# Issuing the attention work beside the FFN by a clock kept while tracing, in an adaLN block on one Trainium2 core

## The chip, the core and the metric

The kernel runs on one core of one Trainium2 chip. The metric is the device time of one execution in microseconds (us). The profile is one execution taken by the hardware profiler. Engines in it: PE (TensorE, matrix products; PEld are its weight loads), DVE (VectorE), ACT (ScalarE), POOL (GpSimd) and SP (SyncE, which here only issues DMAs). Each engine runs its own queue in order; semaphores order engines among each other. In the code they are `pe`, `dve`, `act`, `pool` and `sp`.

## What is computed

The reference, cut to what matters. `x` is 4 x 2048 x 256 (four batches, 2048 positions, 256 features), float32:

```python
mod = silu(c) @ wmod                      # sa, ca, ga, sb, cb, gb per batch
ga, gb = sign(.) * max(abs(.), 0.25)
h = layernorm(x) * (1 + ca) + sa
x = x + ga * attn(h)
h = layernorm(x) * (1 + cb) + sb
x = x + gb * ffn(h)

def ffn(x):                               # weights hold -1, 0, 1
    h = silu(x @ w1.T * w1_s) * (x @ w2.T * w2_s)     # 256 -> 1024
    h = gelu(h @ h1.T * h1_s)                         # 1024 -> 1024
    h = gelu(h @ h2.T * h2_s)
    return h @ w3.T * w3_s                            # 1024 -> 256

# attn: 4 heads of 64, chunks of 64 positions; per chunk and head
A = inv(I + strict(wk @ wk.T * decay))    # wk: unit keys, moved by one position
v_new = A @ v - (A @ wk) @ S
o = (rk * g**p) @ S + intra @ v_new
S = g**64 * S + (wk * g**(63-p)).T @ v_new
return h + (alpha * o) @ Wr.T
```

The state S makes the 32 chunks a chain: a chunk's output, and so its FFN input, needs all chunks before it.

## The kernel before, in words

**Steps and pairs.** A step `s` is one chunk of 64 positions of all four batches and all heads (32 steps); a pair `g` is two steps (16 pairs). The FFN runs over a pair at once (512 columns); in pair 0 it runs over each step by itself (256 columns).

**FFN** (`class Ffn`, L456). `gated` (L511), 8 rounds: four products of PE with `fw1`, four with `fw2` (resident weights) into two PSUM tiles `ps`, Silu on ACT (`sg`), a product on DVE (`raw`). `hidden` (L527), 2 layers of 8 units: 16 products with a weight `w` (512 KB, fetched from DRAM into a ring of three tiles), then Gelu on ACT (`raw`). `last` (L540): 64 products with the resident `fw3`, giving `ps3`; DVE multiplies by gb (`gb`), `store` (L563) adds to `y` and writes out. All activations are split into a rounded part and the rest (`split`, L428: a cast on ACT, a subtraction on DVE or POOL, both written to `act`), so every product is made twice, once with each part: 64 wide products in the gated part of a pair, 256 in the hidden units, 64 half as wide with w3. PSUM tiles of the FFN come from the pool `pf`, three tiles. `Ffn.run` is a generator that yields 88 times: 16 in the gated part, four for each of the 16 hidden units, 8 in the last part. A unit of the plan is the work between two yields.

**Attention, local part** of a step, which needs only x: `load` (DMA of `y`), `local_hidden` (layer norm into `hid`, a square `sq`), `local_sizes` and `local_units` (norms `rn`, unit keys `rk`), `local_residual`, `local_keys` (transposes `tp` on PE, copies `hT` and `keys` on ACT), `local_values` (PE `vp`), `local_reads` (`rkg`), `local_shift` and `local_writes` (`wkg`, by DMA). For a pair: `local_grams` (PE `G`; DVE makes `E` and `IT`; DMAs lay E out anew as `U`), 31 rows `local_inverse` on DVE (two instructions each, `zt` and `Z`), `local_blocks` (DMAs back to `E`), `local_diagonal` (DVE `Dm`), `local_merge1` (PE `yp`, ACT `Y`) and `local_merge2` (PE `ep`, ACT copies to `E`).

**Attention, recurrence** of a step: `rec_state` (PE `R` and `O`, DVE subtracts from `v`, ACT copies `oT`), `rec_values` (PE `V`, ACT `vn`), `rec_update` (PE `new`, DVE `S` and `oT`), `rec_out` (PE `ap`, DVE `ga`, POOL adds to `y`), `ffn_norm` (DVE `bs`, `mv`, `rs`, `xn`; POOL takes the root `rs`) and `ffn_turn` (PE transposes `tpf`, ACT `hm` in 8 instructions, split into `hs`, the input of the FFN). PSUM tiles of these come from two pools, `a2` (two tiles) and `a1` (one tile).

**What sets the order.** The program is traced once; a compile-time scheduler then places the instructions. `stage()` (L105) puts all that is traced inside it behind the last instruction recorded so far on each engine. A class `Engine` (L72) records each instruction in its one `call`, so every line of the profile except that of the set-up's weight check reads L82, and one goes by tile names. In `planned` (L770) each event of the attention is given a number of a unit by hand (`recur`, `local`, `later`); `steps` (L847) walks through the FFN's units and traces the events of a unit, each in a `stage()`, behind it. The FFN's own instructions are in no stage, so the scheduler may move them. The recurrence of pair g + 1 lies beside the FFN of pair g, the local part of later steps beside it too. All DMAs of this part, `w` included, are issued by SP, in one order.

**Set-up** (L572 to L765): loads, the weights' check and rearrangement (`inspect`, `layer`), the tables, and the local part and recurrence of the first steps; then a flag is read and a branch taken (`tc.If`, L871). The path run here is `exact`.

Of the kernel before, what the change touches and what calls it, by code (L numbers as in the profile page):

```python
# [41 lines left out]
C = 64  # L42
# [47 lines left out]
def adaln_block_kernel(ctx: ExitStack, tc: tile.TileContext, x_in, ww, wr, decay, log_alpha, w1, w2, h1, h2, w3, scol,  # L90
# [365 lines left out]
    class Ffn:  # L456
# [6 lines left out]
        def __init__(self, g, i, hs, fp, exact):  # L463
            self.steps, self.fp, self.exact = range(2 * g, 2 * g + 2) if i is None else (2 * g + i,), fp, exact
            self.n = len(self.steps) * B * C
            self.a = hs if i is None else hs[:, :, :, i * B * C:(i + 1) * B * C]
            self.parts = 2 if exact else 1
            self.next, self.new = None, []

        def run(self):  # L470
            for o in range(NH):
                yield from self.gated(o)
            for layer in range(2):
                for o in range(NH):
                    yield from self.hidden(layer, o)
            for i in range(len(self.steps)):
                for n in range(2):
                    yield from self.last(i, n)
# [4 lines left out]
        def fetch(self, src, o):  # L483
            t = self.ring(src.shape[0] // P)
            move(out=t, in_=src[:, o:o + P].rearrange("(k p) o -> p k o", p=P))
            return t
# [24 lines left out]
        def gated(self, o):  # L511
# [12 lines left out]
            self.done(o, to, pool if o < NH - 2 else dve)  # L524
            yield

        def hidden(self, layer, o):  # L527
            ps = pf.tile([P, self.n], F32, tag="f", name="ps2")
            if self.exact:
                w = self.ring(NH)  # L530
                move(out=w.bitcast(F32), in_=fhs[layer][o])
            else:
                w = self.fetch((h1, h2)[layer], o * P)
            yield from self.product(ps, w, 4)
            to = self.acts(o)
            act.activation(to, ps, AF.Gelu, scale=sc[:, 2 + layer, o:o + 1])
            self.done(o, to)
            yield

        def last(self, i, n):  # L540
            if n == 0:
                self.ps = pf.tile([P, 2, D], F32, tag="f", name="ps3")
            at_ = slice((2 * i + n) * P, (2 * i + n + 1) * P)
            for d in (0,) if self.exact else range(0, D, P):
                w = fw3 if self.exact else self.fetch(w3, d)
                count = NH * self.parts
                for m in range(count):
                    k, j = divmod(m, self.parts)
                    pe.matmul(self.ps[:, n, d:d + w.shape[2]], lhsT=self.a[:, k, j, at_], rhs=w[:, k, :],
                              start=m == 0, stop=m == count - 1)  # L550
                    if d == 0 and m == count // 2 - 1:
                        yield
            end = self.steps[i] == NS - 1
            if n == 1 or end:
                m = slice(n, n + 1) if end else slice(0, 2)
                t = ap.tile([P, 2, D], F32, tag="gb", name="gb")
                dve.tensor_tensor(t[:, m], self.ps[:, m], mod[:, GB, m], ALU.mult)
                self.new.append((self.steps[i], t, m))
                if end or self.steps[i] == NS - 2:
                    self.store(dve)  # L560
            yield

        def store(self, eng):  # L563
            s, t, m = self.new.pop(0)
            y = ys[s % 6]
            eng.tensor_tensor(y[:, m], y[:, m], t[:, m], ALU.add)
            for b in range(2):
                rows = out[b::2, s * C:(s + 1) * C, :].rearrange("q t d -> t q d")
                move(out=rows[:, m], in_=y[C * b:C * b + C, m])


    with tc.tile_pool(name="setup", bufs=1) as su:  # L572
# [62 lines left out]
        for h in range(2):  # L635
            move(out=wrT[C * (1 - h):C * (1 - h) + C, 1], in_=wr.rearrange("(k h p) o -> h p k o", h=2, p=C)[h])
        s3b = su.tile([P, D], F32, name="s3b")
# [34 lines left out]
        h0, h1_ = hid, su.tile([P, 2, D], F32, name="hid1")  # L672
# [16 lines left out]
        with stage():  # L689
# [5 lines left out]
            load(2)  # L695
            load(3)
# [11 lines left out]
        with stage():  # L708
# [5 lines left out]
            for j, to in ((2, GA), (5, GB)):  # L714
                for n in range(2):
# [4 lines left out]
                    raw = su.tile([P, D], F32, tag="raw", name="raw", bufs=4)  # L720
# [12 lines left out]
        with stage():  # L733
            for j in range(K - 1):
                local_inverse(j)
            local_residual(0, h0)
            local_residual(1, h1_)
        with stage():
            local_blocks()
        with stage():  # L740
            rn = local_sizes(local_hidden(2, hid))
            local_units(2, hid, rn)
# [6 lines left out]
            local_residual(2, hid)  # L749
# [7 lines left out]
        with stage():  # L757
            oT = rec_update(0, vn, None)
        with stage():
            rec_out(0, oT)  # L760
            ffn_norm(0, xn0)
        some = su.tile([1, 1], F32, name="some")
# [4 lines left out]
    NU = Ffn.UNITS  # L767
    FIRST = 2 * NU - Ffn.LAST

    def planned(exact, hs, fp):  # L770

        plan, had = {}, {"hs": hs}

        def add(u, what, *args, to=None):
            def do():
                got = what(*(had[a[1:]] if isinstance(a, str) else a for a in args))
                if to:
                    had[to] = got

            plan.setdefault(u, []).append(do)  # L780

        def turned(s):
            if s % 2 == 0:
                had["hs"] = new_hs(fp, exact)
            ffn_turn(s, had["xn"], had["hs"], exact)

        def later(u, n):

            for _ in range(n):
                u += 2 if u < FIRST else 1  # L790
            return u

        def recur(s, u):
            add(u, rec_values, s, to="vn")
            add(later(u, 3), rec_update, s, "=vn", "=oT", to="oT")
            add(later(u, 6), rec_out, s, "=oT")
            add(later(u, 10), ffn_norm, s, to="xn")
            add(later(u, 13), turned, s)

        def local(s, u, new=True):  # L800
            if new:
                add(u, local_hidden, s, hid, to="sq")
                add(later(u, 3), local_sizes, "=sq", to="rn")
                add(later(u, 4), local_units, s, hid, "=rn")
                add(later(u, 9), local_residual, s, hid)
            add(later(u, 7), local_shift, s)
            add(later(u, 8), local_keys, s, hid, to="hT")
            add(later(u, 11), local_values, s, "=hT")
            add(later(u, 11), local_reads, s)
            add(later(u, 12), local_writes, s)  # L810

        add(0, rec_state, 1, to="oT")
        recur(1, 8)
        local(2, -12, False)
        u = 4
        for g in range(1, NP):
            a, b = 2 * g, 2 * g + 1

            if g > 1:
                u = later(merge, 6)  # L820
                add(max(u - 18, 0), load, a)
                add(max(u + 2, 0), load, b)
                local(a, u)
                u = later(u, 11)
            local(b, u)
            add(later(u, 12), local_grams)
            u = later(u, 21)
            for j in range(K - 1):
                add(later(u, j // 2 if g == 1 else j * 2 // 3), local_inverse, j)
            u = later(u, K // 2 if g == 1 else (K - 2) * 2 // 3 + 1)  # L830
            add(u, local_blocks)
            merge = max(later(u, 11), FIRST + NU * (g - 2) + 10)

            m = merge
            add(m - 4, rec_state, a, to="oT")
            add(m - 1, local_diagonal)
            add(m, local_merge1, to="Y")
            add(later(m, 3), local_merge2, "=Y")
            recur(a, later(m, 6))
            add(later(m, 12), rec_state, b, to="oT")  # L840
            recur(b, later(m, 16))
        return plan, had

    def new_hs(fp, exact):
        return fp.tile([P, NK, 2 if exact else 1, N], FR if exact else F32, tag="hs", name="hs", bufs=1)

    def steps(exact):  # L847
        for e in engines:
            e.last = None
        with tc.tile_pool(name="ffn", bufs=2) as fp:  # L850
            hs = new_hs(fp, exact)
            with stage():
                ffn_turn(0, xn0, hs, exact)
            plan, had = planned(exact, hs, fp)
            u, f = 0, None
            for g, i in [(0, 0), (0, 1)] + [(g, None) for g in range(1, NP)]:
                before, f = f, Ffn(g, i, had["hs"], fp, exact)
                for n, _ in enumerate(f.run()):
                    if before and n == 17:
                        with stage():  # L860
                            before.store(pool)
                    if i is None and g < NP - 1 and n == NU - 2:
                        with stage():
                            f.store(pool)
                    for what in plan.pop(u, ()):
                        with stage():
                            what()
                    u += 1
            assert not plan, plan
# [33 lines left out]
```

## Time and profile before

| | us |
|---|---|
| median of 3 runs (lowest, highest) | 1963.68 (1962.59, 1964.57) |
| profiled execution, whole | 1957.66 |
| profiled execution, span from first to last instruction | 1955.8 |
| set-up, up to the first product `ps<-hs,fw` | 123.06 |
| pair 0 (two halves) | 123.06 to 263.39 |
| pairs 1 and 2 | 263.39 to 483.24 |
| pairs 3 to 13 | 483.24 to 1755.71 |
| pair 14 | 1755.71 to 1863.55 |
| pair 15, with the last stores | 1863.55 to 1955.8 |

A pair is counted from its first gated product (`ps<-hs,fw`) to that of the next. In the profile's groups a line reads: line, engine, operation, output tile <- input tiles, shapes, count, and in square brackets the idle time of the engine before it with the tile of the instruction that ended it. In the list of waits the numbers are us in total, times, longest. In tables by stretch of time come for PE, PEld, DVE, ACT and POOL the busy us (and instructions), then the granted clock of PE (1.00 is full), the share of the DMA engines' time, and GB/s.

### The profile page before, as it was taken

How to read it: one execution, taken by the hardware profiler on the slowest of the kernel's cores; microseconds unless marked ns; L12 is line 12 of the kernel's file. 1: busy time of each engine (PE TensorE's matmuls, PEld its weight loads, DVE VectorE, ACT ScalarE, POOL GpSimd, SP SyncE). 2: the span in 40 equal slices, each digit the busy share in tenths (PEclk: the TensorE clock that was granted, in tenths of full speed). 3: DMA queues.
4: the chain of work that ended last, by engine and by line, in shares of the span. 5: the costliest groups of instructions: out<-in, count | busy, mean ns of one | idle time of the engine just before them, and what ended most of it. 6: DMA issues, size and time to landing. Idle time of an engine off the chain costs nothing.

```text
span 1955.8 us, 37975 instructions
## 1 busy us (share of the span) xinstructions
PE 1731.8 (89%) x15572; PEld 1405.4 (72%) x15572; DVE 1023.3 (52%) x2426; ACT 813.8 (42%) x1467; POOL 509.2 (26%) x474
## 2 busy tenths in 40 slices
PE   5278889998998989899898998989889898989998
PEld 3068877787776867778676776867778686777876
DVE  3536574555647365564635547363564736456322
ACT  4234444444444344444434334444444444444342
POOL 2222331504124140422404132240412314041020
PEclk7679899999999999999899999999999898999999
DMA  8815535242332425243252423415243252523322
GB/s 281 239 48 188 152 98 151 66 141 71 101 121 76 136 55 139 70 109 116 52 147 67 114 92 87 130 44 151 77 113 94 74 139 52 140 70 101 107 76 88
DMA packets 192216, 213.92 MB, mean 109 GB/s; under 512 B 112864, under 2 KB 147808, under 8 KB 192032
## 3 DMA queue, kind: packets, MB, share of 16 engines
q1 hardware_dynamic: 188096, 199.86, 36.4%
q10 hardware_dynamic: 3936, 11.54, 1.6%
q8 instruction: 125, 2.05, 0.4%
q14 instruction: 59, 0.48, 0.1%
HBM read 177.79 MB, written 25.17 MB: 104 GB/s over the span
## 4 chain that ended last, share of the span: by engine, by line
PE 56%; DVE 14%; DMA 9%; ACT 6%; POOL 4%; SPq 3%; issue 2%; DVEq 0%; POOLq 0%; ACTq 0%
PE ps L82 47%; ACT hm L82 4%; DMA w<-fh 3%; SPq L82 3%; DMA U<-d 3%; DVE Z L82 2%; DVE zt L82 2%; DVE raw L82 2%; DVE xn L82 2%; DMA wkg<-rk 1%; PE vp L82 1%; POOL rn L82 1%; PE new L82 1%; DVE E L82 1%; PE V L82 1%
## 5 line engine op out<-in xcount | busy, mean ns | idle before, releaser
L82 PE MATMUL ps<-act,w 128*128 128x512 f32 (+1 forms) x4352 | 992.2, 384 | 39.3 <-DMA w<-fh 25.9
L82 PEld LDWEIGHTS ps<-act,w 128*128 128x128 f32 x4352 | 780.6, 190 | 202.2 <-ACT act L82 16.7
L82 DVE TENSOR_TENSOR act<-raw,act 128x512 fp32r<-128x512 f32 (+1 forms) x306 | 204.4, 670 | 454.8 <-ACT act L82 436.0
L82 ACT ACTIVATE raw<-ps,sc 128x512 f32<-128x512 f32 (+1 forms) x272 | 178.8, 664 | 448.8 <-PE ps L82 424.3
L82 PE MATMUL ps<-hs,fw 128*128 128x512 f32 (+1 forms) x1088 | 299.0, 432 | 67.7 <-ACT hs L82 33.3
L82 PEld LDWEIGHTS ps<-hs,fw 128*128 128x128 f32 x1088 | 217.6, 214 | 138.9 <-DVE raw L82 44.3
L82 ACT CAST act<-raw 128x512 fp32r<-128x512 f32 (+1 forms) x408 | 240.6, 595 | 129.7 <-DVE raw L82 122.3
L82 POOL TENSOR_TENSOR rn<-rn,half 128x8 f32<-128x8 f32 x32 | 52.6, 1644 | 718.6 <-DVE rn L82 718.6
L82 POOL TENSOR_TENSOR act<-raw,act 128x512 fp32r<-128x512 f32 (+1 forms) x102 | 125.3, 1235 | 249.9 <-ACT act L82 249.9
L82 DVE TENSOR_TENSOR zt<-Z,U 128x126 f32<-128x126 f32 (+22 forms) x496 | 147.8, 298 | 44.7 <-DMA U<-d 32.1
L82 DVE TENSOR_TENSOR Z<-Z,zt 128x126 f32<-128x126 f32 (+22 forms) x496 | 156.2, 315 | 13.5
L82 PE MATMUL ps<-fw,act 128*128 128x256 f32 x1024 | 133.2, 285 | 2.1 <-DVE gb L82 2.0
L82 PEld LDWEIGHTS ps<-fw,act 128*128 128x128 f32 x1024 | 126.5, 189 | 4.6 <-DVE gb L82 2.2
L82 DVE SCALAR_TENSOR_TENSOR raw<-ps,sc,sg 128x512 f32<-128x512 f32 (+1 forms) x136 | 97.1, 715 | 55.2 <-PE ps L82 30.2
L82 ACT ACTIVATE sg<-ps,sc 128x512 f32<-128x512 f32 (+1 forms) x136 | 90.1, 662 | 82.8 <-PE ps L82 82.0
L82 POOL TENSOR_TENSOR rs<-rs,half 128x2 f32<-128x2 f32 x64 | 53.7, 839 | 208.4 <-DVE rs L82 194.1
L82 ACT ACTIVATE hm<-tpf,modT 128x64 f32<-128x64 f32 x256 | 79.4, 417 | 62.6 <-PE tpf L82 62.6
L82 ACT ACT_TABLE_LOAD x38 | 48.8, 1283 | 99.2 <-PE ps L82 90.0
L82 POOL TENSOR_TENSOR y<-y,ga 128x512 f32<-128x512 f32 x32 | 41.2, 1287 | 149.7 <-DVE ga L82 142.5
L82 DVE TENSOR_TENSOR hs<-hm,hs 128x512 fp32r<-128x512 f32 x32 | 26.0, 814 | 101.1 <-ACT hs L82 101.0
L82 PE MATMUL vp<-wwT,hT 128*128 128x256 f32 x256 | 65.1, 390 | 6.6 <-ACT hT L82 5.5
L82 DVE BATCH_NORM_STATS2 bs<-y 128x6 f32<-128x256 f32 x128 | 48.8, 417 | 37.9 <-POOL y L82 31.1
(198 smaller groups left out, 1465.7 us busy)
## 6 DMA issues: line engine op xcount, KB each, us to landing
w<-fh SPq DMA_DIRECT2D x272, 512.0 KB, 3.7
y<-in_x_dram SPq DMA_DIRECT2D x64, 128.0 KB, 4.2
st<-in_h_dram ACTq DMA_DIRECT2D x16, 512.0 KB, 7.2
U<-d SPq DMA_DIRECT2D x32, 256.0 KB, 4.4
fh<-st SPq DMA_DIRECT2D x16, 512.0 KB, 6.8
wkg<-rk SPq DMA_DIRECT2D x64, 126.0 KB
out_dram<-y SPq DMA_DIRECT2D x62, 128.0 KB, 2.4
d<-E SPq DMA_DIRECT2D x64, 64.0 KB, 1.9
```

What stands on the lines that cost most here:

```text
L82: made = make(*args, **kwargs)
```

## The change

The plan by hand goes. In its place, a class `Beside` keeps two clocks while the program is traced, `t` for PE and `dve` for VectorE. Each event has a list of what must be done before it, with a time that must have gone by since (`after`), and a cost on PE, a cost on DVE and the time for which it holds PSUM tiles (`COSTS`). After each unit of the FFN, whose cost is added to the clocks, every event that is ready by the clocks is traced, in the order of a list. The FFN's units are now in stages too, so their instructions stay where they are traced. `w` is issued by ACT, three units ahead (`stream`). `last` makes 14 of 16 products of both steps' first halves before those that need the last activations, and holds both `ps3` tiles at once; the last step is stored whole. In the set-up `load(2)` and `load(3)` come earlier, keys, values and shift of step 2 and hidden and units of step 3 are added, the ring `raw` has 2 tiles for 4, and the flag is read twice.

The diff, cut to its core:

```diff
+            if o > NH - 4:
+                self.stream(o - NH + 3)
             yield
+        def stream(self, m):
+            if self.exact and m < 2 * NH:
+                w = self.ring(NH)
+                self.coming.append(w)
+                act.dma_start(out=w.bitcast(F32), in_=fhs[m // NH][m % NH])
 
         def hidden(self, layer, o):
             ps = pf.tile([P, self.n], F32, tag="f", name="ps2")
-            if self.exact:
-                w = self.ring(NH)
-                move(out=w.bitcast(F32), in_=fhs[layer][o])
-            else:
-                w = self.fetch((h1, h2)[layer], o * P)
+            w = self.coming.pop(0) if self.exact else self.fetch((h1, h2)[layer], o * P)
             yield from self.product(ps, w, 4)
             to = self.acts(o)
             act.activation(to, ps, AF.Gelu, scale=sc[:, 2 + layer, o:o + 1])
             self.done(o, to)
+            self.stream(layer * NH + o + 3)
             yield
...
+        def last(self):
+            steps = range(len(self.steps))
+            ps = [pf.tile([P, 2, D], F32, tag="f", name="ps3") for i in steps]
+            most, count = (NH - 1) * self.parts, NH * self.parts
...
+            for i in steps:
+                if self.exact:
+                    some(i, 0, range(most))
+                yield
+                yield
+            for i in steps:
+                some(i, 0, range(most, count))
+                some(i, 1, range(count))
+                t = ap.tile([P, 2, D], F32, tag="gb", name="gb")
+                dve.tensor_tensor(t, ps[i], mod[:, GB], ALU.mult)
...
+    COSTS = {"state": (1.05, 0.7, (("a2", 2.4), ("a2", 2.4))), "merge1": (0.4, 0, (("a2", 2.2),)),
+             "merge2": (0.55, 0, (("a1", 2.4),)), "V": (0.5, 0, (("a2", 2.0),)), "update": (1.05, 1.7, (("a2", 3.2),)),
+             "out": (1.55, 0.7, (("a1", 2.9),)), "norm": (0, 2.0, ()), "turn": (0.45, 0.75, (("a1", 4.6),)),
+             "hidden": (0, 3.0, ()), "sizes": (0, 0.9, ()), "keys": (0.85, 0.2, (("a2", 3.0),)),
+             "values": (1.55, 0, (("a1", 3.0),)), "grams": (1.15, 2.8, (("a2", 4.2), ("a2", 4.2))),
+             "row": (0, 0.55, ()), "diag": (0, 1.3, ())}
+    class Beside:
...
+        def step(self, s):
+            self.add("state", s, rec_state, (s,), [("update", s - 1, 2.8), ("out", s - 1, 0), ("reads", s, 2.0)], "oT")
+            self.add("V", s, rec_values, (s,), [("merge2", s // 2, 2.8), ("state", s, 2.8), ("values", s, 3.0)], "vn")
+            self.add("update", s, rec_update, (s, "vn", "oT"), [("V", s, 2.5), ("writes", s, 1.5)], "oT")
+            self.add("out", s, rec_out, (s, "oT"), [("update", s, 3.2), ("residual", s, 3.5)])
+            self.add("norm", s, ffn_norm, (s,), [("out", s, 3.6), ("turn", s - 1, 0)], "xn")
+            self.add("turn", s, self.turn, (s, "xn"), [("norm", s, 4.5)] + ([("gated", s // 2 - 1, 0)] if s > 1 else []))
...
+        def ready(self, key, after):
+            if any((k, s) not in self.done for k, s, _ in after):
+                return None
+            t = max([self.done[k, s] + late for k, s, late in after], default=0.0)
+            if key[0] in ("row", "hidden"):
+                t = max(t, self.dve - 0.3)
+            tiles = [k for k, _ in COSTS.get(key[0], (0, 0, ()))[2]]
+            for k in set(tiles):
+                t = max(t, sorted(self.free[k])[tiles.count(k) - 1])
+            return t
...
+        def run(self, until=None):
+            while True:
+                soon = [(r, n) for n, e in enumerate(self.todo[:200]) if (r := self.ready(e[0], e[3])) is not None]
+                now = [n for r, n in soon if r <= self.t]
+                if now:
+                    self.issue(self.todo[now[0]])
+                elif until and until not in self.done:
+                    self.t = min(soon)[0]
+                else:
+                    return
...
+            for g, i in [(0, 0), (0, 1)] + [(g, None) for g in range(1, NP)]:
+                s = 2 * g + (i == 1)
+                beside.run(("turn", 2 * g + (i != 0)))
+                before, f = f, Ffn(g, i, beside.hs, fp, exact)
+                run, n = f.run(), 0
+                while True:
+                    with stage():
+                        if next(run, run) is run:
+                            break
+                    beside.passed(*f.cost(n))
...
+                    beside.run()
+                    n += 1
```

`issue` traces an event in a `stage()` and adds its costs to the clocks; `Ffn.cost` gives a unit 0.92 us on PE (half of it in pair 0) and 0.75 or 1.5 on DVE where it ends a product's chain.

## The prediction

> **What bounds the kernel now.** I read the busy table first, then who PE waits for, then PE in order of time over one pair, then the granted clock.
>
> ```profile
> PE 1731.8 (89%) x15572; PEld 1405.4 (72%) x15572; DVE 1023.3 (52%) x2426; ACT 813.8 (42%) x1467; POOL 509.2 (26%) x474
> ```
>
> PE is the bound, but 89% is an average: 11% of the span is PE idle. The waits of PE say behind what:
>
> ```profile
> PE ps L82 <- DVE raw L82: 42.8, 35, 2.8
> PE yp L82 <- DVE Dm L82: 36.0, 2, 35.1
> PE ps L82 <- ACT hs L82: 33.3, 15, 3.3
> PE tpf L82 <- DVE xn L82: 28.5, 25, 1.6
> PE ps L82 <- DMA w<-fh: 25.9, 16, 3.3
> ```
>
> The second is one wait in the set-up. The other four (130.5 us) return in every pair of steps, about 8.7 us each time. In time order, around the change from one FFN to the next:
>
> ```profile
> 1000.27 0.83 PE L82 MATMUL yp<-Dm,E 32*32 32x32 f32 x64
> 1001.03 5.30 PE L82 MATMUL ps<-act,w 128*128 128x512 f32 x22
> 1006.27 1.20 PE L82 MATMUL ep<-E,Y 32*32 32x32 f32 x64
> ...
> 1055.98 0.55 PE L82 MATMUL tpf<-kept,xn 128*128 128x128 f32 x3 [0.95 <-DVE xn L82]
> 1056.46 1.16 PE L82 MATMUL G<-keys 64*64 64x65 f32 x64
> 1059.75 0.73 PE L82 MATMUL ps<-hs,fw 128*128 128x512 f32 x2 [2.13 <-ACT hs L82]
> ...
> 1074.73 7.50 PE L82 MATMUL ps<-hs,fw 128*128 128x512 f32 x24 [2.04 <-DVE raw L82]
> 1082.89 11.18 PE L82 MATMUL ps<-act,w 128*128 128x512 f32 x48 [0.65 <-DVE raw L82]
> 1097.12 3.23 PE L82 MATMUL ps<-act,w 128*128 128x512 f32 x13 [3.05 <-DMA w<-fh]
> ```
>
> The recurrence (yp to tpf) begins in the FFN's ninth of 16 hidden units (3 + 87/16 after its first), takes 56 us, and its last transpose comes after the FFN's last product. So PE stands until xn, then hs, are there. Then the gated products wait for DVE, which runs rows of the inverse between them, and then a weight is late. The clock falls in such holes:
>
> ```profile
> 1016.00:1024.00 8.00, 8.00 (x96) 6.46 (x95) 3.62 (x7) 2.62 (x4) 1.45 (x1) 1.00 0.36 93
> 1056.00:1064.00 8.00, 5.63 (x79) 4.04 (x80) 4.27 (x7) 5.07 (x11) 3.94 (x6) 0.86 0.13 22
> 1072.00:1080.00 8.00, 5.96 (x19) 3.92 (x19) 7.62 (x19) 3.54 (x6) 2.79 (x3) 0.79 0.00 0
> 483.24:1755.71 1272.47, 1163.86 (x10472) 940.87 (x10473) 692.32 (x1618) 532.09 (x947) 350.46 (x320) 0.97 0.36 99
> ```
>
> (Third from last is the granted clock.) The last line is pairs 3 to 13, from first gated product to first gated product: 1272.47/11 = 115.7 us a pair.
>
> **The price of a dense pair.** Pair 15 has nothing beside it and gives the FFN alone:
>
> ```profile
> 1880.14 40.41 PE L82 MATMUL ps<-act,w 128*128 128x512 f32 x176
> 1939.00 5.86 PE L82 MATMUL ps<-fw,act 128*128 128x256 f32 x48
> ```
>
> 0.2296 us a wide product, 0.122 a w3 product. A pair has 64 + 256 wide and 64 of w3: 73.5 + 7.8 = 81.3 us. The events beside it: from 1000.27 to 1038.68 stand 121 wide products (27.8) and yp, ep, V, new, ap, R/O, tp, V, vp, so these nine cost 10.6 with their switches. From 1038.68 to 1050.09 stand 64 w3 products (7.8) and tpf, new, half a tp, ap: 3.6. Left are half a tp (0.4), vp (1.7), tpf (0.6), G (1.2), R/O (1.1): 5.0. Together 19.2, so 100.5 us a pair if PE never waits. Today's 115.7 has 15.2 on top: some 10 idle, the rest products stretched by waits and low clock.
>
> **Part by part.** *The order.* The changed kernel's issue order is visible. From pair 3 on PE has tp at unit 10, yp inside 10, ep at its end, V in 11, new, ap, R/O in 12, V and tp in 13, G and the first tpf behind 13, ap in 15, the second tpf after 28 of the 64 w3 products. After it come 36 x 0.122 = 4.4 us of work. The turn (hm 2.48, hs cast 0.62, handovers about 0.1 each) gives the first half of hs 3.3 us after tpf and the second (DVE 0.69) about 4.2. So both hs waits, the xn wait and the cold start go. What is late next, taken through the queues at those durations:
> - V waits for E, whose copy (1.16 in two, about 10 us into the unit 10 stretch) stands on ACT behind sq and Gelu: 0.5.
> - ap waits for oT; S and oT (0.87, 0.68) stand on DVE behind the unit's act: 0.5.
> - G needs both PSUM tiles of its pool. One is freed by S and oT of step b, behind xn of step a, which took 2.69 where POOL ran beside it (0.73 otherwise): 0 to 1.4, taken 1.4.
> - The first rows of the inverse stand on DVE ahead of hs. They need U, 8.8 us after E in the trace; some 10.8 after G, with 17 available: nothing, with 6 us of slack.
>
> *Rows in the gated part* are now one per pair of products: stt 0.75 + row about 0.5 in 1.84 us of PE, done before the POOL split starts, where zt and Z took 1.1 to 1.4 against 0.28. I cost them at 0; with that cover gone it is today's 2 to 4 us.
>
> *w on ACT, three ahead.* w leaves the SP queue, where a late y or wkg held it. Its issue stands on ACT between Gelu and cast: 13 in the hidden units. ACT's issues of the same 512 KB in the set-up took 0.34 and 0.45 alone, 0.66 each in four (2.63), 1.38 each in six (8.29). I take 0.5. At a layer's end the chain Gelu, issue, cast, DVE act is 0.25 + 0.69 + 0.5 + 0.62 + 0.69 + 0.1 = 2.9 against 14 products x 0.23 = 3.2 that don't need it: covered; at 1.38 it costs 0.6 twice. The first w of a pair is issued behind the sixth Silu, at about 11.4, lands at 3.7 (median) to 4.9, and is wanted at 14.7: 0.4 to 1.6, taken 0.6, at most today's 3.05. Boundaries and gb before its PSUM tile returns: 0.5.
>
> Waits: 0.5 + 0.5 + 1.4 + 0.6 + 0.5 = 3.5 (bounds 0.5 and 9). **A steady pair: 104.0.**
>
> *last()* computes 28 products before it needs the last act (3.4 us against 2.9): the wait goes.
>
> A rule beside the clock rows: the Trainium skill ("TensorE: Matmul & The Clock Gate", Part 1) has the array drop to half rate after about 3.4 us of idle and return after about as long of work. The trace agrees in kind: pair 15, started out of a 3.2 us wait, took 16.6 us for its 64 gated products instead of 14.7. By the rule, waits of half a microsecond keep the clock up; the sum above has that already.
>
> **The other stages.** Set-up: 123.06 us to the first FFN product. Work of steps 2 and 3 moves in. Hidden 2 lies partly in DVE's idle time before 63.5, where the rows still wait for the check of the weights; 1.7 us of it fall between rows, hidden 3 takes its old place, values 2 lie in PE's idle 4.7 before tpf. The second flag load is over long before. 123.5 (121 to 127).
> Pair 0 (140.3, in halves of 256 columns) is paced by w: a slot comes back with the last product, then Silu/Gelu 0.47, issue 0.5, landing 3.7 to 4.5, and 16 x 0.127 = 2.0: three units in 6.7 to 7.5, so 2.4 each. First half: gated 8 and its events 10, 16 x 2.4 = 38, rest 6: 62. Second: gated 10, nine units 21.6, seven at 2.0 with 15 of events, and its end 13 with the turn open: 74. Together **136** (129 to 142).
> Here the Trainium skill ("DMA: Bandwidth & Descriptors", "Issuing engines are not separate DMA queues") speaks against the move: an issue from another engine saves only issue time. If so and pair 0 kept its 140.3, the total would be 4 higher. The trace leaves it open, with w on one queue only.
> Pairs 1 and 2 still have a late second tpf: 100.5 + 3.5 + cold start 1.9 + open turn 4.3 = 110.2, and 2.1 open: 108.0. Pair 14 has no tp, vp, G: 100.5 - 6.1 + 3.5 + 4.3 = 102.2. Pair 15: 16.6 + 58.8 + 0.5 + 7.8, then gb, y and the store as today (7.3): 91.0.
> Sum: 123.5 + 136 + 110.2 + 108 + 11 x 104 + 102.2 + 91 = 1814.9 us of span. The profiled execution had 1.86 around its span (1957.66), and the median stands at 1963.68/1957.66 = 1.0031 of it: (1814.9 + 1.9) x 1.0031 = **1822 us**.
>
> **Rivals.**
> - *Nearly dense*: waits of 0.5 a pair, pair 0 at 131, set-up 121.5: 1773. For it: slack at U, hs, tp. Against: ACT and DVE are in order and the four waits above are each real queue positions.
> - *The clock kept in tracing runs ahead of the chip.* It counts 16.1 us of PE for events that cost 19.2 here, and no queues of ACT or POOL. PE then waits at more of the 17 events: 9 a pair instead of 3.5, pair 0 as today: 1904. Against: a clock that runs short on PE gives inputs more time, not less.
> - *Slower*: ACT becomes the bound. If an issue on ACT holds the engine until the transfer before it has drained, it costs about a landing, 3.7, and a unit takes 0.69 + 0.62 + 3.7 = 5.0 instead of 3.68: 13 x 1.33 = 17.3 a pair, 57 in pair 0, 2139 in all. It outweighs the gain of 11.7 from 3.3 us an issue. For it: 1.38 at six in a row; against: 0.34 to 0.66 otherwise, and w is issued one per 3.7 us.
> - *It moves nothing*: the holes close and open elsewhere for the same 115.7. Against: order and durations above leave no place for 15 us.
>
> **Chances.** Forecast (waits 2 to 5; 1800 to 1845) 0.55; nearly dense 0.15; clock ahead 0.20; moves nothing 0.04; ACT bound 0.06. A difference under 0.2% can't be told from no change here. Faster 0.90, same 0.02, slower 0.08. The range for 8 in 10 takes in most of the second and third case: 1778 to 1890.
>
> **What would show it.** hs and xn gone from PE's waits; gated products at 0.23; clock 1.00 through a pair; pairs at 102 to 106; w waits under 1 us; ACT issues near 0.5. Wrong if PE waits for E, oT or G's tiles by more than 2 us each, if DVE rows still hold raw, or if ACT queue time grows past 1 us an issue.

## The result, and the profile after

The kernel after takes 1868.41 us (median of 4 runs, 1866.87 to 1870.42); the kernel before, run beside it, 1963.13 (1961.39 to 1964.57). The ratio is 0.9518, with a 95% interval of 0.9502 to 0.9535: 4.8% faster. The forecast was 1822, the range 1778 to 1890. So the direction held and the size fell short by 46 us. The profiled execution took 1866.87, its span is 1865.1.

The busy table of the kernel after (busy us and share of the span for each engine):

```profile
PE 1704.2 (91%) x15572; PEld 1375.3 (74%) x15572; DVE 1002.9 (54%) x2424; ACT 816.8 (44%) x1467; POOL 528.5 (28%) x474
```

PE does the same 15572 instructions in 27.6 us less busy time, and its idle time falls from 224 to 161 us. The waits of PE over the whole span:

```profile
PE V L82 <- DVE v L82: 18.1, 13, 2.4
...
PE ps L82 <- ACT hs L82: 12.9, 5, 3.2
...
PE tpf L82 <- DVE xn L82: 7.8, 2, 6.4
```

The counts matter here: `hs` fell from 15 waits to 5 and `xn` from 25 to 2, all outside the ten steady pairs looked at below. In their place `V` waits, once a pair for `E` and once for `v`. By stages (pair 0, then pairs 3 to 13; third from last the granted clock):

```profile
124.58:280.69 156.11, 129.92 (x1524) 118.31 (x1524) 76.48 (x204) 67.30 (x154) 43.31 (x47) 0.91 0.44 131
...
501.82:1675.75 1173.93, 1134.71 (x10472) 912.29 (x10473) 678.97 (x1616) 533.86 (x947) 367.14 (x318) 1.00 0.39 107
```

Pairs 3 to 13, the steady pairs, take 1173.93/11 = 106.7 us each in place of 115.7, and the clock stays at 1.00. The gain is there: 11 x 9.0 = 99. Pair 14 (1675.75 to 1773.82) gives 9.8 more. Pair 0 takes back 15.8 (156.1 against 140.3). One steady pair of the kernel after in PE's order of time, from the `V` that waits for `E` to the start of the next pair:

```profile
1101.49 0.69 PE L82 MATMUL V<-v,E 64*64 64x64 f32 x32 [0.74 <-ACT E L82]
...
1115.40 0.69 PE L82 MATMUL V<-v,E 64*64 64x64 f32 x32 [1.47 <-DVE v L82]
...
1134.77 3.49 PE L82 MATMUL ps<-fw,act 128*128 128x256 f32 x28
1138.10 0.60 PE L82 MATMUL tpf<-kept,xn 128*128 128x128 f32 x4
1138.45 4.47 PE L82 MATMUL ps<-fw,act 128*128 128x256 f32 x36
1142.76 1.10 PE L82 MATMUL ps<-hs,fw 128*128 128x512 f32 x4
```

Behind the last transposes 36 w3 products still run; in these 4.47 us `hm` and `hs` get done, and the first gated product starts without a wait. In before the same transposes came after the FFN's last product.

Where does a steady pair lose what is left? The waits of PE in ten pairs (607.5 to 1675.8):

```profile
PE V L82 <- DVE v L82: 15.3, 10, 2.4
PE V L82 <- ACT E L82: 8.2, 10, 0.9
PE ps L82 <- ACT act L82: 4.6, 10, 0.5
PE ps L82 <- DMA w<-fh: 3.2, 6, 0.9
```

With 2.2 for `act` of VectorE and 1.6 for `raw` these are 35.1 us, 3.5 a pair. Besides, the 64 gated products of a pair take 17.07 us from the first to the first product of the next layer, not the 14.7 that they need at full rate; about 0.5 of the 2.4 us between are the waits for `raw` and the first `w`, which the 35.1 hold already. ACT in that part, two rounds of it:

```profile
1041.07 0.69 ACT L82 ACTIVATE sg<-ps,sc 128x512 f32<-128x512 f32 x1
1042.57 0.62 ACT L82 CAST act<-raw 128x512 fp32r<-128x512 f32 x1 [0.82 <-DVE raw L82]
1043.10 0.68 ACT L82 ACTIVATE sg<-ps,sc 128x512 f32<-128x512 f32 x1
1044.60 0.62 ACT L82 CAST act<-raw 128x512 fp32r<-128x512 f32 x1 [0.82 <-DVE raw L82]
```

The clock is 1.00, yet a round takes 2.03 us from Silu to Silu (the next two 2.02 and 2.11) where PE needs 8 x 0.2296 = 1.84. The Silu `sg` of a round stands behind the cast of the round before it; that cast waits for VectorE's product `raw`, and `raw` needs `sg`. Product, cast, Silu go round in series. That reading is an inference until an experiment cuts the loop.

### The profile page after: what moved, and what is told of

Same layout as the page of the kernel before. It is cut to its first block, busy times and chain, and to the rows that moved or that the text cites. A ratio compares the mean times of both kernels' runs of the same rounds, so it can differ in the third digit from the quotient of the medians.

```text
span 1865.1 us, 37816 instructions
## 1 busy us (share of the span) xinstructions
PE 1704.2 (91%) x15572; PEld 1375.3 (74%) x15572; DVE 1002.9 (54%) x2424; ACT 816.8 (44%) x1467; POOL 528.5 (28%) x474
## 3 DMA queue, kind: packets, MB, share of 16 engines
q8 instruction: 124, 2.03, 0.5%
## 4 chain that ended last, share of the span: by engine, by line
PE 64%; DVE 8%; ACT 7%; DMA 6%; POOL 4%; issue 3%; SPq 1%; ACTq 0%; POOLq 0%; DVEq 0%
PE ps L82 52%; PE vp L82 3%; DMA w<-fh 3%; ACT hm L82 2%; DMA wkg<-rk 2%; PE new L82 2%; POOL y L82 2%; ACT act L82 2%; ACT raw L82 2%; DVE hid L82 2%; PE V L82 1%; POOL rs L82 1%; PE tp L82 1%; DVE raw L82 1%; POOL gh L82 1%
## 5 line engine op out<-in xcount | busy, mean ns | idle before, releaser
L82 PEld LDWEIGHTS ps<-act,w 128*128 128x128 f32 x4352 | 779.2, 190 | 187.6 <-ACT act L82 15.3
L82 DVE TENSOR_TENSOR act<-raw,act 128x512 fp32r<-128x512 f32 (+1 forms) x306 | 231.5, 756 | 461.1 <-ACT act L82 460.5
L82 PE MATMUL ps<-hs,fw 128*128 128x512 f32 (+1 forms) x1088 | 271.7, 399 | 20.5 <-ACT hs L82 12.9
L82 PEld LDWEIGHTS ps<-hs,fw 128*128 128x128 f32 x1088 | 192.8, 192 | 94.0 <-ACT sg L82 28.9
L82 DVE TENSOR_TENSOR zt<-Z,U 128x126 f32<-128x126 f32 (+22 forms) x496 | 136.9, 276 | 9.0 <-DMA U<-d 0.5
L82 PE MATMUL ps<-fw,act 128*128 128x256 f32 x1024 | 127.7, 282 | 0.0
L82 ACT ACTIVATE sq<-hid 128x512 f32<-128x512 f32 x32 | 20.2, 632 | 134.0 <-DVE hid L82 134.0
L82 POOL TENSOR_TENSOR rk<-hid,rn 128x512 f32<-128x512 f32 x32 | 34.1, 1067 | 138.0 <-DMA wkg<-rk 136.8
L82 POOL TENSOR_TENSOR y<-y,gb 128x512 f32<-128x512 f32 x30 | 39.9, 1331 | 96.9 <-DVE gb L82 96.9
L82 POOL TENSOR_TENSOR wkg<-wkg,gtail 128x512 f32<-128x512 f32 x32 | 42.5, 1327 | 85.1 <-DMA wkg<-rk 49.7
```

The lines of the kernel that those rows point to most:

```text
L82: made = make(*args, **kwargs)
```

## The experiments

The theory after the result: (1) the gain comes from the order, the FFN in its traced places with events put between its units; (2) what is lacking against the forecast is the loop in the gated part, `V`'s wait for `v`, and pair 0. The main rivals: the gain is that of w on its own queue; or what is lacking is the kept clock's own error. Each kernel ran with the kernel before on the same chip. Before took 1961.68, 1951.2, 1962.96 and 1954.65 us in the four groups (first four kernels, next four, next three, last one), so ratios carry the verdict, and periods of steady pairs the mechanism. A ratio is a kernel's time over that of before in its group, with the 95% interval in brackets. The kernel after itself did not run again in these groups.

### w issued by SP again

```diff
-                act.dma_start(out=w.bitcast(F32), in_=fhs[m // NH][m % NH])
+                move(out=w.bitcast(F32), in_=fhs[m // NH][m % NH])
```

> The kernel after, with the w transfers still issued three units ahead, but by SP, where they stand behind the transfers of the events, and not by ACT. Theory (the order of the work makes the gain, and the queue of w matters little, since an event is now issued when its inputs are nearly there, so that SP seldom stands at a transfer that waits): +5 to +20 us on the 1868.4 of after, that is 1873 to 1888, with w waits of some 0.5 to 1.5 us a pair on PE in place of 0.3. Rival (the gain came from freeing w of SP's queue): what before lost to w waits comes back and more, +26 us or over, 1894 or more.

Ratio 0.9662 (0.9629 to 0.9695) against 0.9518: 1.5% slower than after, about 28 us (21.5 between the two profiled spans). The time itself, 1891.3, lies between the two ranges. By the ratio the loss has the rival's size, but not its place. A steady pair takes 106.75 us, as after; the w waits rise from 3.2 to 9.6 in ten pairs and other waits shrink. Most of the loss is in pair 0 (166.8 against 156.1) and pair 1 (117.8 against 111.6), where single w waits reach 7.1 and 4.3 us: SP stands at the transfers `E<-d` (till 224.31 and 349.34 us) and issues the w behind them at 228.19 and 353.22. So the queue of w matters only where the events are not yet in step.

### Before, with w on ACT

```diff
+            if o > NH - 4:
+                self.stream(o - NH + 3)
             yield
...
-                move(out=w.bitcast(F32), in_=fhs[layer][o])
...
+            w = self.coming.pop(0) if self.exact else self.fetch((h1, h2)[layer], o * P)
...
             self.done(o, to)
+            self.stream(layer * NH + o + 3)
```

> The kernel before, with its plan and its free scheduling, but with the w transfers issued by ACT three units ahead, as the change does. Theory (this part alone is worth the w waits of before and no more, 25.9 us in the whole trace): 1937 to 1958. Rival (the part is the larger half of the gain of 95): 1916 or less.

Ratio 1.0009 (0.9994 to 1.0025): nothing. The w waits of ten steady pairs fall from 19.5 to 4.3 and `xn`'s from 25.3 to 2.0, but `raw`'s rise from 28.5 to 37.5 and 16.4 appear for `act`; a steady pair gains 0.9 us, and pair 0 gives 5.2 back. Both the theory's 5 to 26 us and the rival fall: freed of w, PE stands at other waits of the same order.

### The FFN free to move

```diff
-                    with stage():
-                        if next(run, run) is run:
-                            break
+                    if next(run, run) is run:
+                        break
```

> The kernel after, but the units of the FFN are free for the scheduler to move, as they were in before; the events are issued at the same places of the trace. Theory (the kept clock is worth something only if the order that it was kept for is the order that runs): most of the gain goes, 1910 to 1960, and the holes ahead of R, V, new and ap of 1 to 2 us each come back. Rival (the places of the events are what counts, and the scheduler keeps to them well enough): 1862 to 1885.

Ratio 1.0207 (1.0173 to 1.0241): slower than before, beyond the theory's range. A steady pair takes 116.5 us. In its trace the layers run ahead, the recurrence of both steps comes late, partly among the w3 products, and in ten steady pairs PE waits 75.2 us for `xn` and 32.1 for `hs`, 10.7 a pair. The kept clock is worth nothing by itself: its places are times in an order of the FFN, and hold only with that order. The reverse was not run: the plan by hand with the FFN in stages, or the new `last` alone. So how the gain divides between the fixed order of the FFN, the kept clock's places and `last` is open; the next two runs show only what other places cost.

### The table's PE costs times 1.25, and times 0.8

The edit multiplies the first number of each entry of `COSTS`, for `state` 1.05 to 1.312, or to 0.84.

> The kernel after, with the PE costs of all events in the table times 1.25: the table says 16.1 us of PE for the events of a pair, the trace of after has some 20.0, so that the kept clock falls 3.9 us a pair behind. Theory (the waits after that are left, 3.5 us a pair, do not come from the clock being short, but from queues that it does not know: VectorE behind POOL's y, ACT's order in the gated part): within 0.4 per cent, 1861 to 1876, the steady pair 106.0 to 107.2. Rival (the shortness misplaces the events): at least half of the 3.5 us of waits goes or as much comes, 30 us either way, 1840 or 1898.

Ratio 0.9839 (0.9804 to 0.9873), a steady pair 112.4 us. The theory falls, and the rival's loss of 30 us is exceeded.

> The kernel after, with the PE costs of all events in the table times 0.8, where times 1.25 gave 0.9839 of before in place of 0.9518 and a steady pair of 112.4 us in place of 106.7. Theory (a short clock is a margin: it holds events back longer than the table's latencies say, so that PE finds them ready): no loss, the steady pair 105.5 to 107.0, ratio 0.945 to 0.953. Rival (any other table loses, since the latencies were found together with these costs, and events that slip past a boundary wait for the next): the steady pair 108 or more, 0.96 or more.

Ratio 0.9873 (0.9853 to 0.9892), a steady pair 111.9 us. This theory falls too; the rival holds. Both directions lose two thirds or more of the gain. At times 1.25 yp and ep come to lie inside the gated part, where PE waits for `raw` (up to 6.3 us at once); at 0.8 the last transposes come after the last w3 product, and `hs` is waited for (32.1 us in ten pairs), as in before.

### Cast behind the next Silu

```diff
                     act.activation(sg, ps, AF.Silu, scale=sc[:, 0, o:o + 1])
                     yield
+                    if o > 0:
+                        self.done(*self.late)
...
-            self.done(o, to, pool if o < NH - 2 else dve)
+            self.late = o, to, pool if o < NH - 2 else dve
+            if o == NH - 1:
+                self.done(*self.late)
```

> The kernel after, but in the gated part the cast of a unit's result (ACT) and its remainder (POOL or VectorE) are traced one unit later, behind the Silu of the next unit. Nothing is left out. Theory (the 16.7 us of the gated part in a steady pair, in place of 14.7, are a loop: product on VectorE, cast on ACT, Silu of the next unit behind it on ACT, product again, 2.05 us a round against 1.84 of PE): the loop is cut, the gated part falls to 14.7 to 15.2 us, 1.5 to 2.0 a pair, 24 to 32 us in all, 1836 to 1846. Rival (gated products of 512 columns simply cost 0.26 us each): no change, 1864 to 1873. A third outcome: the cast that comes later makes the layer boundary later, and part is given back there.

Ratio 0.9458 (0.9430 to 0.9486), 0.6% below after; a steady pair 105.4 us, the gated part 15.83 in place of 17.07. ACT in the kernel with this edit:

```profile
1038.98 0.69 ACT L82 ACTIVATE sg<-ps,sc 128x512 f32<-128x512 f32 x1 [0.67 <-PE ps L82]
1039.57 0.61 ACT L82 CAST act<-raw 128x512 fp32r<-128x512 f32 x1
1040.85 0.69 ACT L82 ACTIVATE sg<-ps,sc 128x512 f32<-128x512 f32 x1 [0.67 <-PE ps L82]
```

Now the Silu waits for PE, and a round takes 1.87 us: the loop was the limit, and PE is now. So the mechanism is shown; of the expected 1.5 to 2.0 us a pair, 1.3 came. Of the rest the trace shows one place: in an early round the two instructions of one row of the inverse took 1.15 and 1.24 us on VectorE, where those of the row before took 0.23 and 0.24; the product behind them came late, and PE waited 0.39 us for `raw`.

### ga in another buffer

```diff
-        t = ap.tile([P, 2, D], F32, tag="tmp", name="ga")
+        t = ap.tile([P, 2, D], F32, tag="hm", name="ga")
```

The chain that it tests, in the kernel after, on POOL and then on VectorE:

```profile
1110.36 1.04 POOL L82 TENSOR_TENSOR rk<-hid,rn 128x512 f32<-128x512 f32 x1 [6.28 <-DMA wkg<-rk]
...
1112.73 1.30 POOL L82 TENSOR_TENSOR y<-y,gh 128x512 f32<-128x512 f32 x1
```

```profile
1114.06 0.69 DVE L82 TENSOR_TENSOR ga<-ap__11698,mod 128x512 f32<-128x512 f32 x1 [5.55 <-POOL y L82]
1114.67 0.68 DVE L82 TENSOR_TENSOR v<-v,R 128x512 f32<-128x512 f32 x1
```

> The kernel after, but the product ga of the attention's output no longer shares its buffer with gh of the local part; it takes that of hm, which lies idle at the time. No instruction changes its place. Theory (V of the second step waits 1.5 us a pair for v, because ga, ahead of v on VectorE, waits for POOL to give the shared buffer back, and POOL stood 6.3 us for the wkg transfer): the 15.3 us of V's waits for v in ten steady pairs fall under 3, 1.2 to 1.5 a pair, 17 to 24 us in all, 1844 to 1852. Rival (POOL's y of the step before is needed anyway soon after, and PE waits for norm or hs in its place): the wait moves to another row and the time stays at 1864 to 1873.

Ratio 0.9454 (0.9427 to 0.9481), 0.7% below after, some 13 us by the ratio. A steady pair takes 104.8 us in place of 106.7, 21 us in eleven pairs; before itself was 12 us faster in this group, which makes its ratio the smaller measure. The row of `V`'s waits for `v`, 15.3 us in ten pairs, is gone. A buffer shared with a slow engine was the cause: PE, VectorE and POOL run the same instructions in the same order as in after.

### The first w earlier

```diff
-            if o > NH - 4:
-                self.stream(o - NH + 3)
+            if o < 3:
+                self.stream(o)
```

> The kernel after, but the first three w transfers of a pair are issued in the first three rounds of the gated part and not in its last three. Theory (pair 0 took 156.1 us in place of 136 in part because its stream began only at 144.7 us, 2.1 us ahead of the first product that needed it, so that its w waits of 10.4 us fell there): pair 0 falls by 8 to 12 us, the first w waits of the steady pairs (0.3 us a pair) go, 1852 to 1860. Rival (in pair 0 the transfers are slow, as the second half's layers run at the pace of the stream and not of its start): pair 0 loses 0 to 4 us, 1863 to 1869.

Ratio 0.9501 (0.9476 to 0.9527): not to be told from after by ratios. Pair 0 falls from 156.1 to 154.1 only; its w waits go from 10.4 to 6.4, and `raw` takes 3.5 of that. So the rival holds for pair 0. The steady pair falls to 105.7, more than expected, by a side effect: in the first four rounds ACT now runs Silu ahead of the cast of the round before (gated part 16.28). I infer why: the issue is recorded as ACT's last instruction of a unit, so the next unit is tied behind it and no longer behind the cast. This kernel cuts part of the same loop, so most of its gain in a steady pair is not a gain from w.

### All three

> The kernel after with all three edits at once: the cast one unit later, ga in the buffer of hm, the first three w transfers in the first three gated rounds. Theory (three separate losses, which add): 1836 to 1846 less 17 to 24 less 8 to 12, that is 1800 to 1820, the steady pair 102.7 to 103.7 us. Rival (they hide one another): the largest single gain and little more, 1832 to 1845.

Ratio 0.9351 (0.9325 to 0.9376), 1825.08 us: the fastest of all here, 1.8% below after. The first of its waits of PE in ten pairs, and the same ten pairs as one stretch:

```profile
PE V L82 <- ACT E L82: 8.0, 10, 0.9
```

```profile
595.30:1633.41 1038.11, 1018.61 (x9522) 832.28 (x9521) 639.30 (x1471) 485.80 (x861) 332.94 (x290) 1.00 0.38 110
```

`V`'s wait for `E` is what is left with a name of its own (the others are 4.7 for `raw`, 4.6 and 2.3 for `act`). 103.8 us a pair, 2.9 below after, where the three alone gave 1.3, 2.0 and 1.0. The sum of 4.3 is not reached; the first and the third act on the same loop. The time lies between the theory's range and the rival's, and the steady pair misses the theory's by 0.1. Pair 0 falls to 147.1.

### Two edits on top of the three

In pair 0 a unit of 256 columns gets its true cost on PE in the kept clock, and 0.6 in place of half of a unit's cost on VectorE:

```diff
-            part = len(self.steps) / 2
+            part = 0.6 if len(self.steps) == 1 else 1.0
```

> The kernel with all three edits, in which a unit of the first pair's halves (256 columns) costs the kept clock 0.55 us and not 0.46: the trace has 2.14 us for 16 of its matmuls, so 0.535 a unit, at full clock. It has 0.9351 of the time of before without this edit. Theory (in pair 0 the kept clock lags by a sixth, so that rows and merges of pair 1 are issued late and the second turn of the pair stands 6.4 us for xn at its end): pair 0 falls by 4 to 8 us of its 147.1, the ratio to 0.931 to 0.933; the steady pair stays at 103.8. Rival (pair 0 is paced by the w transfers and by the granted clock, 0.90 and 0.96 in its halves, and by the latency of the chain): pair 0 within 2 us, 0.934 to 0.936.

Ratio 0.9696 (0.9677 to 0.9715); pair 0 takes 153.7 us, 6.6 more. The theory falls: taking away the lag of the kept clock does not mend pair 0. Unexpectedly pairs 3 to 13 take 110.1 each: yp now lies in the gated part of each. PE there:

```profile
1065.65 0.78 PE L82 MATMUL yp<-Dm,E 32*32 32x32 f32 x64
...
1073.36 2.07 PE L82 MATMUL ps<-hs,fw 128*128 128x512 f32 x4 [4.86 <-DVE raw L82]
```

> The kernel with all three edits, in which V is held back 4.0 us behind merge2 in the kept clock and not 2.8, since the trace has V waiting 0.8 us in every pair for the copy of E on ACT, where sq and a Gelu stand ahead of it. It has 0.9351 of the time of before without this edit. Theory (what is left of the waits in a steady pair are latencies that the table puts too low, and PE has FFN work to do meanwhile): the steady pair loses those 0.8 us, 103.8 to 103.0, ratio 0.931 to 0.933. Rival (the rest of the pair's chain moves with V and ends late): the steady pair 104 or more, 0.936 or more.

(The edit replaces 2.8 behind `merge2` by 4.0 in the list of `V`.) Ratio 0.9887 (0.9866 to 0.9909), a steady pair 113.0 us. The rival holds, far beyond its 104. PE at the end of a pair of this kernel, and the table by stretches of 4, 6 and 2 us around it (from 1174 on the clock is 1.00):

```profile
1156.19 6.13 PE L82 MATMUL ps<-fw,act 128*128 128x256 f32 x50
1162.17 0.60 PE L82 MATMUL tpf<-kept,xn 128*128 128x128 f32 x4
1166.04 2.37 PE L82 MATMUL ps<-hs,fw 128*128 128x512 f32 x4 [3.27 <-ACT hs L82]
```

```profile
1162.00:1166.00 4.00, 0.77 (x7) 0.53 (x6) 1.34 (x4) 3.09 (x9) 0.32 (x1) 0.94 0.31 68
1166.00:1172.00 6.00, 5.96 (x13) 4.42 (x14) 2.13 (x6) 2.11 (x3) 0.00 (x0) 0.50 0.45 131
1172.00:1174.00 2.00, 2.00 (x9) 1.62 (x8) 0.84 (x2) 1.05 (x2) 0.87 (x1) 0.91 0.49 111
```

The transposes now stand behind the last w3 product instead of 36 products ahead of it. After the wait of 3.27 us for `hs` the clock is at 0.50 for about 6.8 us (0.5 before 1166, 6.0, 0.4 after 1172, by the shares below 1.00), and the gated part grows by 1.8, from 15.90 to 17.68. With `ep` waiting 2.0 for `Y`, and `act` and `tp` 0.8 and 0.7 longer, less the 0.8 that `V` no longer waits, this gives 7.8 of the 9.2 us by which a pair grew.

### E copied by VectorE

```diff
-            act.copy(E[r, :, :, K:C], ep[r])
+            dve.tensor_copy(E[r, :, :, K:C], ep[r])
```

> The kernel with all three edits (0.9351 of before), in which the two copies of merge2's result into E are made by VectorE and not by ACT; every event keeps the place that the kept clock gave it. Theory (V waits 0.8 us a pair because these copies stand on ACT behind sq, which itself waits 3.3 us for hid, and behind a Gelu, while VectorE has nothing from 1071.8 to 1074.2; holding V back in the kept clock failed because it moved all that follows, not because the wait cannot go): the waits of V for E, 8.0 us in ten pairs, fall under 1, the steady pair from 103.8 to 103.0 to 103.2, ratio 0.930 to 0.933. Rival (the same place is taken by a later wait, for v or act, or the copies delay the cast behind hid): the steady pair stays at 103.6 to 104.0, ratio 0.934 to 0.937.

Ratio 0.9451 (0.9433 to 0.9468), a steady pair 105.8 us: worse by 1% than the three edits alone. Neither text foresaw it. VectorE in this kernel:

```profile
1084.70 0.69 DVE L82 TENSOR_TENSOR act<-raw,act 128x512 fp32r<-128x512 f32 x1 [2.07 <-ACT act L82]
1085.31 1.39 DVE L82 COPY E<-ep 32x512 f32<-32x512 f32 x2
```

The copies stand behind the remainder `act` in VectorE's order, which waits 2.07 us for ACT's cast, and that cast is behind `sq` as before. They end at 1086.70, and `V` starts at 1086.80. The wait of `V` grew from 0.8 to about 2.0 us (19.7 in ten pairs, in a row that names no releaser). This is 1.2 of the 2.0 us by which a pair grew; the rest is the clock, which goes to 0.50 for 3.41 us in five of the ten pairs: these take 106.6, the others 105.0 (one 105.7). Another engine does not help when its own order leads back to the same wait.

## Why the prediction was right or wrong

**The order: right.** The waits for `xn` and `hs` are gone from steady pairs, the clock is 1.00, and 36 w3 products of 4.47 us (forecast 4.4) cover the turn. That this, and not w's queue, is the gain is shown by the free FFN (slower than before, with the same events) and by w on ACT alone (no change); how much of it the new `last` brings was not run.

**The steady pair: 104.0 forecast, 106.7 measured; the term that failed is the price of the FFN.** The forecast took 64 gated products at 0.2296 us, 14.7, and put the 16.6 of pair 15 down to a cold clock. That row was read rightly. Pair 15 of before in three stretches, and ACT in the last of them:

```profile
1863.55:1867.20 3.65, 3.65 (x9) 2.89 (x10) 0.67 (x1) 1.93 (x2) 0.00 (x0) 0.54 0.00 0
1867.20:1870.60 3.40, 3.40 (x16) 2.70 (x16) 1.50 (x2) 1.43 (x3) 1.30 (x1) 0.99 0.00 0
1870.60:1880.14 9.54, 9.54 (x42) 7.58 (x41) 3.76 (x5) 6.46 (x12) 6.99 (x6) 1.00 0.00 1
```

```profile
1874.29 0.68 ACT L82 ACTIVATE sg<-ps,sc 128x512 f32<-128x512 f32 x1
1875.74 0.69 ACT L82 ACTIVATE sg<-ps,sc 128x512 f32<-128x512 f32 x1 [0.77 <-PE ps L82]
1876.33 0.61 ACT L82 CAST act<-raw 128x512 fp32r<-128x512 f32 x1
1877.49 0.63 ACT L82 CAST act<-raw 128x512 fp32r<-128x512 f32 x1 [0.56 <-DVE raw L82]
1878.02 0.68 ACT L82 ACTIVATE sg<-ps,sc 128x512 f32<-128x512 f32 x1
```

After the cold start two Silus run ahead of two casts, and two rounds take 3.73 us, close to PE's 3.67. But that is the order of a scheduler that is free to move the FFN's units. The change puts these units in stages, and with them each Silu behind the cast of the round before. So the step that failed is that a price from the free order was carried over to the fixed one. In the kernel after the 64 products take 17.07 us at full clock, 2.4 more than 14.7. Some 0.5 of this are the waits for `raw` and `w` counted in the next paragraph. Most of the other 1.9 is the loop of Silu, product and cast, which is there in pair 15 too, where nothing stands beside the FFN (2.03 to 2.09 us from Silu to Silu at clock 1.00). With the FFN free, Silus go in twos again; with the cast moved, the 64 products take 15.8 (0.4 of it a wait for `raw`), so the loop accounts for 1.1 of the 1.9, and the rest stays unexplained. The remaining 0.8 lies in the events' price: 20.1 us by PE's busy time, with 19.2 forecast.

**The waits: 3.5 forecast and 3.5 measured, by other terms.** `V` for `E` 0.8 (0.5 forecast); `ap` for `oT` 0 (0.5); G's tiles 0 (1.4); the first w 0.3 (0.6); boundaries and gb 0.8 (0.5). Instead `V` of the second step waits 1.5 for `v`, which the forecast had not seen: it had followed the queues of the engines, but not the one buffer shared by gh and ga. That the sum agrees is chance.

**w on ACT: right, mis-sized.** An issue takes 0.33 us, not 0.5, and in the pair looked at it starts 0.03 to 0.14 us into a running ACTIVATE or cast, so it costs ACT nearly nothing there. The rival "ACT becomes the bound" is refuted. The rule of the Trainium skill ("DMA: Bandwidth & Descriptors", "Issuing engines are not separate DMA queues") that another issuing engine saves only issue time agrees with the steady pairs, 106.7 with either issuer. Of the 10.7 and 6.3 us that pairs 0 and 1 lost with SP, w waits of PE are 5.1 and 4.3. The two longest of them come from SP's order: it stood at event transfers whose data were not there, which is no matter of bandwidth.

**Pair 0: 136 forecast, 156.1 measured, the largest miss of a single pair (20 us; the eleven steady pairs together missed by 30).** The forecast let it gain by the pace of w. By its own parts, over both halves, the gated parts took 37.5 us in place of 28, the hidden units 96.9 in place of 89, and the ends 21.7 in place of 19. The end of the second half in the kernel after:

```profile
270.00:280.00 10.00, 1.14 (x4) 0.69 (x4) 5.84 (x19) 3.10 (x9) 4.08 (x4) 0.64 0.18 52
280.00:290.00 10.00, 8.81 (x31) 6.79 (x32) 3.81 (x10) 5.21 (x8) 4.88 (x5) 0.67 0.00 0
```

There PE stands for `xn` and `hs`, and the clock falls. Over the whole of pair 0, against before, PE's time without work grows from 13.9 to 26.2 us (10.4 of it for w, 6.4 for `xn` of the second turn), and its busy time from 126.5 to 129.9, at 0.91 in place of 0.94. The loop accounts for about 5.7 (cast behind the next Silu: 150.4), the late start of w for about 2. The 6.4 for `xn` stayed in all of w by SP, the three edits alone and together, and E on VectorE; with the true cost of half units 6.1 for `v` and 3.2 for `xn` came in its place. Why the chain to the second turn is late there stays open.

**The other stages.** Set-up 124.6 (123.5 forecast), pairs 1 and 2 111.6 and 109.6 (110.2 and 108.0), pair 15 91.3 (91.0). Pair 14 took 98.1 in place of 102.2: the open turn came (3.21 us for `hs` at its end, 4.3 forecast), but the 3.5 us of other waits did not; PE's idle time in it is 3.4 in all.

**The rival of the kept clock** had 0.20, with 9 us of waits a pair. The kernel after is not that case. But the argument against it, that a clock running short gives inputs more time and does no harm, is refuted: with costs times 0.8 the pair takes 111.9 us, and the last transposes come after the last w3 product. I read it so that the chain of events is about as long as the pair, and what comes late misses its end; what was run shows the loss, not the length of the chain. Changed costs on PE lost 5.1 us a pair (times 0.8) and 5.7 (times 1.25), one changed latency 9.2. At times 1.25 the costs of a pair add up to 20.1 us, which is what the trace shows; so truer numbers did not make a faster kernel here.

## What to carry to other kernels

When a wait is removed by ordering, look next for loops through two in-order engines (here Silu, product, cast) and for buffers shared with a slow engine: neither is seen by pricing the instructions, and cutting them gave 1.8% more. The times written into such a schedule need not have a smooth optimum: a change of 1.2 us in one latency cost 9 us a pair here, so measure each such number on the chip. A price read off a kernel holds for the order in which it ran; where a change also fixes that order, price it again. A place found for an event is only worth something with the order of the main work that it was found in.

## What was not expected of the hardware

A PE wait of 3.27 us was followed by a granted clock of 0.50 from 1165.53 to 1172.36 (the run with `V` held back), so a hole costs more than its length. In each trace here, from pair 0 to pair 14, the stretches at 0.50 begin on one grid with a step of 3.41 us and last whole steps: one in the kernel after (795.10 to 798.51), two here, three in the run with the true cost of half units (629.15 to 639.39). So a shorter hole can do it as well, if it lies badly to the grid. In the kernel after, nine steady pairs have `V` waiting about 1.4 us for `v` and keep 1.00; in the tenth it waited 2.43, PE was busy for 0.97 us of the step from 791.70 to 795.10, the next step was at 0.50, and that pair took 109.3 us. With E copied by VectorE all ten pairs have nearly the same wait of 2.0 us, and five of them a step at 0.50. The Trainium skill ("TensorE: Matmul & The Clock Gate", Part 1) gives about 3.4 us for the fall and for the return; the step agrees, but here 2.43 us of waiting were once enough for a fall, and the return after 3.27 took two steps.

A DMA issue on ACT (0.33 us) runs beside the ACTIVATE ahead of it: issued at 1052.38 while the Silu of 1052.30 to 1052.99 ran, with the cast following at 1052.88.
